# A selective scan inside a four-layer network: outputs kept in the gathered tiles and scattered through four views, gathers moved to the head of each step, last rows written from three tiles

## The chip, the cores and the metric

The kernel runs on one core of a Trainium2 chip. The metric is the device time of one execution in microseconds (us), the median of several runs. The core has five engines that work side by side, each through its own queue in order: PE (TensorE, matmuls), DVE (VectorE), ACT (ScalarE), POOL (GpSimd) and SP (SyncE, which here only issues DMAs). An instruction waits at the head of its queue until the semaphores it needs are up, and everything behind it on that engine waits too.

## The reference, cut to what matters

The input is one image of 1024 channels and 64 x 64 = 4096 pixels. Four residual layers follow, each `x = x + layer(groupnorm(x))`: a mixing layer with a decay along the channels (L0), a 1x1 convolution (L1), a gated state-space layer (L2), another 1x1 convolution (L3). The change lies in L2:

```python
xz = silu(in_proj_w @ x + in_proj_b)            # 3072 channels
x_ssm, res, gate = split(xz, 3)                 # 1024 each
xf = silu(depthwise_conv3(x_ssm))               # along the 4096 pixels
dt, B, C = split(dbc_w @ xf + dbc_b)            # per head: 1, 8 and 8 rows; dt = softplus(dt)
x_h, dt, B, C = gather(..., perm[head])         # pixels in another order, per head
for t in pixels:                                # state h: 512 x 8 per head
    h = exp(dt[t] * A) * h + dt[t] * B[t] * x_h[t]
    y[t] = h @ C[t]
y = gather(y + D * x_h, inverse(perm))          # back to the pixels' order
out = silu(out_proj_w @ (y * silu(gate) + res) + out_proj_b)
```

There are 2 heads of 512 channels and 8 states.

## The kernel before, in words

All 1024 x 1024 products are done by a seven-product scheme on halves of the matrices (`multiply`): per pair of pixel blocks, two groups of seven products, each product two half-products of 8 matmul records. Their operands are the normalized image (`b11`, `b21`, `b22`, from ACT at L943) and differences of it (`t1` to `t4`, made at L797 by DVE or POOL).

**The stage before the scan (WX).** The x_ssm product runs over four pairs of blocks. `conv` (L1054) and `turn` (L1075) follow it: each block is convolved, transposed and written as 512-byte pieces of rows to the DRAM tensor `tok_d` (L1098), one row per pixel and head: 512 channels, then the parts of C and B and dt. `finish(pair)` (L1144) takes the dt, B and C of one pair of blocks from `acc`: softplus of dt, B times dt (L1185), and then, for every lot of four 128-pixel tiles, the split of B and C into a high and a low part (L1198, L1200 on DVE; the second copies L1201, L1202 on POOL) into one tile `row`, which is written to `tok_d` by SP (L1205 to L1210). There is a single `row`, so the next lot's first write (L1191 on DVE) waits until the DMA of the lot before has landed. Between two lots of a pair the generator yields once, that is for one product's time; in the last pair (`finish(NP - 1)`, nine tiles: two lots of four and one of one) there is nothing between.

**The scan.** The 4096 pixels of each head are taken in 74 chunks (`NK`) of 56 pixels, the two heads in one tile of 128 partitions. For each chunk k:
- `gather(k)` (L1289): an indirect DMA from POOL brings 128 rows of `tok_d` into the tile `g` (6 buffers). It is asked for at the end of step k - 5.
- `step_sums`, `turn_rows`, `spread_decay`: `ds` on ACT (L1299), two small products `pr` on PE (L1305, L1306), then `bts`, `E`, `cd` on DVE (L1312 to L1320).
- `cross` (L1327, `pg` on PE), the Exp of `E` on ACT (L1384), `weigh` (L1335, L1337, L1340: the 128 x 128 matrix `G` on DVE).
- `apply(k)`: `py = G' g` on PE (L1344); ACT copies the 8 state rows of each head from `py` into the next chunk's `g` (L1347), and all of `py` into a tile `y` with 2 buffers (L1349). `py` has one PSUM buffer.
- `scatter(k)` (L1353): an indirect DMA from POOL writes `y` to rows of `y_d`. `y_d` is one DRAM tile, and as its rows are chosen at run time each scatter is ordered behind the one before: POOL waits until that one has landed.

Between these the PE is given the half-products of the next product, WR (`res`), by `next_units`: one or two in each turn of the loop `for k in range(-1, NK + 1)` (76 turns). Eight matmul records make a half-product. Its results go through `rg` tiles: ACT copies them out (L1024), DVE adds (L1028), ACT applies silu four at a time (`activate`, L1034) and SP writes them to `res_d`. 14 half-products are given before the first turn of the loop. `sums`, one piece a turn, forms combinations of two weight matrices on POOL (L468 to L488) with loads and stores on SP (L475, L484, L495).

The order on DVE, PE, POOL and ACT is the order of the program text (`manual_schedule`). The pools of the scan stage (`l2r2` with 6 `rg` tiles, `l2g`, `l2b`, `l2h`) lie where the pools of the WX stage (`l2a`, `l2a2`) lay, so their first writers wait for the last users of those.

After the scan, `two_steps` computes gate, out_proj and L3; `load_y` (L1498) reads `y_d`.

Of the kernel before, what the change touches and what calls it, by code (L numbers as in the profile page):

```python
# [36 lines left out]
NK = -(-N // LT)  # L37
HS = HEADS * S
KW, MW = 4 * HS, 66
NF2 = 9 * HS  # L40
CF, BF, DT = 0, KW, 2 * KW
HI, LO = {CF: (0, 2), BF: (0, 1)}, {CF: (1, 3), BF: (2, 3)}
NSPEC = HEADS * S + 1

W1, WX, WR, WG, WO, W3 = range(6)
# [47 lines left out]
def tile_net(ctx: ExitStack, tc: tile.TileContext, x, par_d, cst_d, w_d, w2_d, dbcw_d, out):  # L93
# [17 lines left out]
    s2_d = {m: dram.tile([7, 7, P, 2 * QO], F32, name=f"s2_{m}_d") for m in (WG, WO, W3)}  # L111
    res_d = dram.tile([C, N], F32, name="res_d")
    tok_d = dram.tile([HEADS * N + NSPEC, DH + NF2], F32, name="tok_d")
    y_d = dram.tile([HEADS * N + P * NK, DH], F32, name="y_d")
    perm_d = dram.tile([HEADS * N, 1], I32, name="perm_d")


# [113 lines left out]
    with tc.tile_pool(name="spec", bufs=1) as sp:  # L231
        rows = sp.tile([NSPEC, DH + NF2], F32, name="spec")
        nc.gpsimd.memset(rows, 0.0)
        for at in (BF, CF):
            for j in HI[at]:
# [265 lines left out]


    mean0 = const.tile([P, CT], F32, name="mean0")
    sum0 = const.tile([P, CT, 2 * NPIECE], F32, name="sum0")
    sq0 = const.tile([P, CT, 2 * NPIECE], F32, name="sq0")
    with tc.issue_after(exp_ln.ins), tc.tile_pool(name="l0x", bufs=2) as lx, \
            tc.tile_pool(name="l0x2", bufs=1) as lx2, \
            tc.tile_pool(name="wsum0", bufs=1, side="right") as wsum0, \
# [30 lines left out]
        for t in range(T0):  # L539
            nc.gpsimd.tensor_scalar(dtm[:, t, :], cst[:, CST["row"]], pcol("dtw", t), None, ALU.mult)  # L540
        carry = l0.tile([P, 2, T0], F32, name="carry", bufs=1)
        nc.vector.memset(sum0, 0.0)
        nc.vector.memset(sq0, 0.0)
        nmean0 = l0.tile([P, CT], F32, name="nmean0", bufs=1)
# [494 lines left out]
    with tc.tile_pool(name="l2a", bufs=2) as pa, tc.tile_pool(name="l2a2", bufs=1) as pa2, \  # L1039
# [104 lines left out]
        def finish(pair):  # L1144
            n = 2 * TPB
            yield
            acc = accs[pair].rearrange("p b (h f) -> p b h f", h=HEADS)
            if pair == NP - 1:

                nc.vector.memset(acc[:, n], 0.0)  # L1150
                nc.scalar.activation(end, end, AF.Silu)
                pe = ps_tp("end_pt")
                nc.tensor.transpose(pe[:CT, :P], end, ident)
                et = pa.tile([CT, P], F32, name="end_t", bufs=1)
                nc.scalar.copy(et, pe[:CT, :P])
                for h in range(HEADS):
                    nc.sync.dma_start(tok_d[h * N + N - 1 : h * N + N, :DH].rearrange("a (b c) -> (a b) c", c=P),
                                      et[h * KH : (h + 1) * KH, :])
                pz = ps_tp("end_dbc")
                for o in range(CT):  # L1160
                    nc.tensor.matmul(pz[:1, : HEADS * NF], end[:, o : o + 1], both[:, o, P:], start=(o == 0), stop=(o == CT - 1))
                nc.vector.tensor_tensor(accs[pair][:1, n], pz[:1, : HEADS * NF], dbcb[:1], ALU.add)
                n += 1


            def t(name):
                w = pa.tile([P, 2 * TPB + 1, HEADS], F32, tag=f"sp_{name}", name=f"sp_{name}{pair}", bufs=1)
# [12 lines left out]
            nc.vector.reciprocal(v, u)  # L1180
            nc.vector.tensor_tensor(d, d, v, ALU.mult)
            nc.scalar.activation(u, u, AF.Ln)
            nc.vector.tensor_tensor(u, u, d, ALU.add)
            nc.vector.tensor_tensor(u, u, m, ALU.add)
            nc.vector.tensor_tensor(f[:, :, :, 1 : 1 + S], f[:, :, :, 1 : 1 + S],  # L1185
                                    u.unsqueeze(3).to_broadcast([P, n, HEADS, S]), ALU.mult)
            for b0 in range(0, n, TPB):
                if b0:
                    yield
                q = min(TPB, n - b0)  # L1190
                nc.vector.tensor_copy(row[:, :q, :, DT], u[:, b0 : b0 + q])  # L1191
                for h in range(HEADS):
                    for at, c in ((BF, 1), (CF, 1 + S)):
                        v = f[:, b0 : b0 + q, h, c : c + S]
                        parts = row[:, :q, h, at : at + KW].rearrange(
                            "p b (a c) -> p b a c", c=HS)[:, :, :, h * S : (h + 1) * S]
                        (hi, hi2), (lo, lo2) = ([parts[:, :, j] for j in which[at]] for which in (HI, LO))
                        nc.vector.tensor_scalar(hi.bitcast(I32), v.bitcast(I32), 12, 12, ALU.logical_shift_right,  # L1198
                                                ALU.logical_shift_left)
                        nc.vector.tensor_tensor(lo, v, hi, ALU.subtract)  # L1200
                        nc.gpsimd.tensor_copy(hi2, hi)  # L1201
                        nc.gpsimd.tensor_copy(lo2, lo)  # L1202
                    t0 = pair * 2 * FB + b0 * P - 1
                    if t0 < 0:
                        nc.sync.dma_start(tok_d[h * N : h * N + P - 1, DH:], row[1:, 0, h, :])  # L1205
                        nc.sync.dma_start(tok_rows(t0 + P, q - 1, NF2, DH, h), row[:, 1:q, h, :])
                    elif q < TPB:
                        nc.sync.dma_start(tok_d[h * N + N - 1 : h * N + N, DH:], row[:1, 0, h, :])
                    else:
                        nc.sync.dma_start(tok_rows(t0, q, NF2, DH, h), row[:, :q, h, :])  # L1210

        forget(LATE)
        with tc.manual_schedule(engines={E_.DVE, E_.PE, E_.Pool, E_.Activation}):
# [47 lines left out]
            while ready or due or due2 or due3:  # L1261
                follow()
                next_units(8)
                next_units(8)
                follow_on()
                next_units(8)
                activate(len(silus))
            for _ in finish(NP - 1):
                pass

# [3 lines left out]

    with tc.tile_pool(name="l2r2", bufs=6) as prg, tc.tile_pool(name="l2g", bufs=6) as pgat, tc.tile_pool(name="l2b", bufs=2) as pb, tc.tile_pool(name="l2h", bufs=1) as ph, \
            tc.tile_pool(name="ps2b", bufs=1, space=PSUM) as psb:
        rg_pools[:] = [prg] * 6 + rg_pools * 4
        G2 = [ph.tile([P, P], F32, name=f"G{i}") for i in range(2)]  # L1280
# [60 lines left out]

        def apply(k):
            py = psb.tile([P, FB], F32, tag="y", name=f"py{k}")
            nc.tensor.matmul(py, G2[k % 2], rows.pop(k)[:, :DH], start=True, stop=True)  # L1344
            if k + 1 < NK:
                for h in range(HEADS):
                    nc.scalar.copy(rows[k + 1][h * LC : h * LC + S, :DH], py[h * LC : h * LC + S])  # L1347
            y = pb.tile([P, DH], F32, tag="y", name=f"y{k}")
            nc.scalar.copy(y, py)  # L1349
            return y  # L1350

        def scatter(k, y):
            nc.gpsimd.indirect_dma_start(  # L1353
                out=y_d[:, :], out_offset=bass.IndirectOffsetOnAxis(ap=dst_[:, k : k + 1], axis=0),
                in_=y[:, :], in_offset=None,
            )

        sums = (None for m in (WO, W3) for _ in sum_weights2(m, ph, nc.sync, 64, lag=(1, None)))
# [3 lines left out]

        pgs = {}
        with tc.manual_schedule(engines={E_.DVE, E_.PE, E_.Pool, E_.Activation}):
            while given < first:
                next_units(total)
            for k in range(5):
                gather(k)
            step_sums(0)
            for k in range(-1, NK + 1):  # L1370
                upto = first + (k + 2) * (total - first) // (NK + 2)
                turned = turn_rows(k + 1) if k + 1 < NK else None
                if k > 0:
                    weigh(k - 1, pgs.pop(k - 1))
# [446 lines left out]
```

## Time and profile before

| | |
|---|---|
| median of 3 runs | 2718.75 us (2718.61 to 2720.78) |
| the profiled execution | 2721.77 us, span 2719.4 us |
| PE / DVE / ACT / POOL busy | 95% / 67% / 40% / 45% of the span |
| DMA | 598.22 MB, mean 220 GB/s |
| scan stage, 1142.54 to 1649.50 us | 506.96 us, PE busy 482.92, DVE 365.57, ACT 325.29, POOL 311.88 |
| `g` gathers, `y_d` scatters | 74 each, 964 and 1012 ns on POOL each |

In the group and timeline lines, `out<-in` are the program's names, `x74` a count; the brackets or the last columns hold the idle time of the engine just before and what ended it. An ended wait is named by the instruction or the DMA that came last. A timeline line can hold several instructions, merged. "PEclk" is the share of full clock that PE was granted in a stretch.

### The profile page before, as it was taken

Reading aid. Unit: us, or ns where it says so; the run is one execution under the profiler, and the core shown is the slowest. Engines: PE = TensorE matmul, PEld = TensorE weight load, DVE = VectorE, ACT = ScalarE, POOL = GpSimd, SP = SyncE. Lnnn points to the kernel's source line nnn. Section 1 sums busy time; section 2 is a strip of 40 time slices with the busy share of each in tenths; the row PEclk is TensorE's granted clock in tenths of the full one; section 3 lists DMA queues with packets and bytes.
Section 4 is the critical chain, followed back from the end, with each engine's and each line's share of the span. In section 5 each row is a group of like instructions: output and inputs, shape, how many; then the busy total and the mean of one; then the engine's idle time right before and its main releaser. Section 6 shows DMA issues by size and latency. Waiting matters only on the chain.

```text
span 2719.4 us, 30951 instructions
## 1 busy us (share of the span) xinstructions
PE 2577.5 (95%) x9520; PEld 1715.8 (63%) x9520; DVE 1824.2 (67%) x3870; ACT 1086.4 (40%) x1840; POOL 1223.9 (45%) x1166
## 2 busy tenths in 40 slices
PE   4788999999999999999999999999999999999999
PEld 3664444444555555444444447888888888788887
DVE  6996856655555644377777775577576686877777
ACT  3783110103646554375766554322233133321220
POOL 4154123232122220246585665566575565654544
PEclk9897999999999999999999999999999999999999
DMA  7245467546443363478888994879799898788896
GB/s 287 102 169 201 147 218 262 190 124 230 139 138 103 110 175 111 144 236 262 236 236 236 277 269 152 242 244 305 217 278 292 235 308 238 248 304 292 299 328 215
DMA packets 423577, 598.22 MB, mean 220 GB/s; under 512 B 141909, under 2 KB 211669, under 8 KB 420342
## 3 DMA queue, kind: packets, MB, share of 16 engines
q1 hardware_dynamic: 299062, 368.89, 42.3%
q10 hardware_dynamic: 91456, 136.33, 14.3%
q0 software_dynamic: 32896, 91.04, 12.9%
q8 instruction: 77, 1.26, 0.2%
q14 instruction: 86, 0.70, 0.1%
HBM read 435.63 MB, written 160.51 MB: 219 GB/s over the span
## 4 chain that ended last, share of the span: by engine, by line
PE 48%; DVE 3%; DMA 2%; issue 2%; ACT 2%; POOL 1%; SPq 0%; DVEq 0%; POOLq 0%; ACTq 0%
PE mm L839 8%; PE q_P2P L1695 5%; PE q_P6P L1695 5%; PE q_P5P L1695 5%; PE q_P3P L1695 5%; PE q_P7P L1695 5%; PE q_P1P L1695 5%; PE q_P4P L1695 5%; PE py L1344 2%; DMA y_d<-y,dst 1%; POOL s L468 1%; PE pr L1305 1%; DMA g<-tok_d,src 0%; DVE pg L1337 0%; DVE t L797 0%
## 5 line engine op out<-in xcount | busy, mean ns | idle before, releaser
L839 PE MATMUL mm<-t,w 128*128 128x512 f32 x1536 | 687.4, 598 | 9.3 <-ACT rg L1024 6.2
L839 PE MATMUL mm<-b,w 128*128 128x512 f32 x1152 | 518.7, 602 | 4.0 <-ACT b L943 2.9
L839 PEld LDWEIGHTS mm<-t,w 128*128 128x128 f32 x1536 | 287.4, 191 | 335.2 <-issue 315.6
L839 PEld LDWEIGHTS mm<-b,w 128*128 128x128 f32 x1152 | 218.0, 193 | 254.7 <-issue 243.7
L1664 ACT COPY qQ<-q_P5P 128x512 f32<-128x512 f32 x48 | 28.1, 585 | 294.9 <-PE q_P5P L1695 294.9
L1065 DVE SCALAR_TENSOR_TENSOR cvp<-xs,par,cvp 128x512 f32<-128x512 f32 x128 | 95.3, 754 | 71.7 <-ACT cvp L1062 69.4
L1353 POOL DMA_INDIRECT y_d<-y,dst x74 | 74.9, 1012 | 143.2 <-ACT y L1349 83.5
L468 POOL TENSOR_TENSOR s<-s 128x256 f32<-128x256 f32 (+3 forms) x120 | 130.0, 1090 | 7.9
L1092 POOL TENSOR_TENSOR acc<-l2xt,acc 128x136 f32<-128x136 f32 x56 | 27.2, 486 | 234.6 <-ACT l2xt L1086 233.6
L1116 DVE TENSOR_TENSOR xs<-mm,xs 128x512 f32<-128x512 f32 x64 | 41.9, 685 | 125.0 <-PE mm L839 125.0
L1347 ACT COPY g<-py 8x512 f32<-8x512 f32 x146 | 83.6, 573 | 77.4 <-PE py L1344 69.5
L958 DVE SCALAR_TENSOR_TENSOR image<-mm,par,image 128x512 f32<-128x512 f32 x64 | 47.2, 746 | 95.6 <-PE mm L839 95.6
L1084 PEld LDWEIGHTS l2pt<-both,cv 128*128 128x128 f32 x512 | 77.6, 192 | 34.6 <-issue 24.2
L1335 DVE TENSOR_TENSOR E<-E,pg 128x512 f32<-128x512 f32 x74 | 50.5, 683 | 69.1 <-PE pg L1327 63.5
L797 POOL TENSOR_TENSOR t<-t,b 128x512 f32<-128x512 f32 x40 | 55.6, 1416 | 90.7 <-DVE t L797 90.6
L943 ACT ACTIVATE b<-image,gnl_bias,gnl_r_r 128x512 f32<-128x512 f32 x48 | 36.9, 807 | 143.8 <-PE mm L839 122.4
L1695 PE MATMUL q_P1P<-t_b,wq_P1P 128*128 128x256 f32 x384 | 92.5, 385 | 1.9 <-POOL t_b L1459 1.9
L1463 ACT ACTIVATE qb<-x_x_b,gn_bias,gn_r_r 128x512 f32<-128x512 f32 x64 | 48.8, 807 | 109.2 <-DVE qQ L1625 37.3
L1695 PE MATMUL q_P4P<-t_t,wq_P4P 128*128 128x256 f32 x384 | 90.9, 380 | 1.3 <-DVE qV L1672 1.3
L797 POOL TENSOR_TENSOR t<-b,t 128x512 f32<-128x512 f32 x60 | 76.2, 1294 | 35.4 <-DVE t L797 35.3
L1695 PE MATMUL q_P5P<-t_t,wq_P5P 128*128 128x256 f32 x384 | 90.8, 379 | 0.0
L1695 PE MATMUL q_P6P<-t_t,wq_P6P 128*128 128x256 f32 x384 | 90.7, 379 | 0.0
(418 smaller groups left out, 5972.5 us busy)
## 6 DMA issues: line engine op xcount, KB each, us to landing
w<-s_d SPq DMA_DIRECT2D x96, 512.0 KB
w<-in_w_dram SPq DMA_DIRECT2D x72, 512.0 KB
x_x_b<-x_d ACTq DMA_DIRECT2D x28, 1024.0 KB
image<-x_d SPq DMA_DIRECT2D x12, 2048.0 KB
wq_P6P<-s_d SPq DMA_DIRECT2D x84, 256.0 KB
wq_P7P<-s_d SPq DMA_DIRECT2D x84, 256.0 KB
wq_P5P<-s_d SPq DMA_DIRECT2D x84, 256.0 KB
wq_P3P<-s_d SPq DMA_DIRECT2D x84, 256.0 KB
```

Of the source, the lines that this page charges most:

```text
L468: eng.tensor_tensor(out, a, b, ALU.subtract)
L797: eng.tensor_tensor(B[name][k], B[one][k], B[two][k], ALU.subtract)
L839: nc.tensor.matmul(to[o], w[:, k, o * P : (o + 1) * P], B[name][k], start=(fresh and k == 0), stop=(k == KH - 1), skip_group_check=True)
L958: nc.vector.scalar_tensor_tensor(part, ps, pcol(bias_name, o), part, ALU.add, ALU.add)
L1065: nc.vector.scalar_tensor_tensor(cv, xo[:, at + t : at + t + FB], pcol("dww", 3 * o + t), cv, ALU.mult, ALU.add)
L1084: nc.tensor.matmul(pt[:, q * NV : (q + 1) * NV], cv[:, (q0 + q) * P : (q0 + q + 1) * P], both[:, o, :], start=True, stop=True)
L1335: nc.vector.tensor_tensor(Ef, Ef, pg, ALU.mult)
L1344: nc.tensor.matmul(py, G2[k % 2], rows.pop(k)[:, :DH], start=True, stop=True)
L1347: nc.scalar.copy(rows[k + 1][h * LC : h * LC + S, :DH], py[h * LC : h * LC + S])
L1353: nc.gpsimd.indirect_dma_start(out=y_d[:, :], out_offset=bass.IndirectOffsetOnAxis(ap=dst_[:, k : k + 1], axis=0), in_=y[:, :], in_offset= ...
L1463: nc.scalar.activation(tile_of(j, name)[:, k], held[j, "x", name][:, k], AF.Identity, bias=bias, scale=scale)
L1695: nc.tensor.matmul(ps[:, o, :], w[:, k, o * P : (o + 1) * P], rhs[:, k, :], start=(new and o == 0 and k == 0), stop=(k == 1), skip_group_c ...
```

## The change

1. `y_d` becomes a DRAM tensor outside the pools, and the scatters write in turn through four views of it that the dependency tracker takes as disjoint: a scatter is no longer ordered behind the one before. (Reads of `y_d` still are behind all of them.)
2. `apply` copies `py` into the first 512 columns of the gathered tile `g` of its own chunk, which nothing reads any more; the tile `y` is gone. `g` has 8 buffers for 6. So `gather(k + 5)`, which takes over the tile of chunk k - 3, is behind `scatter(k - 3)`.
3. `gather(k + 5)` stands at the head of turn k, before `turn_rows`, not at the end behind `scatter(k - 1)`; the first five stand before the half-products that are given ahead of the loop (13 for 14), with one `activate(4)` among these.
4. In `finish`, the split of C comes before the softplus, that of B after it; both copies of a part are written by one DVE instruction (its input is broadcast), so the POOL copies are gone. Between two lots of a pair there are two yields for one. In the last pair the lots are 4, 3 and 2 tiles, each in a tile of its own (`row`, and two `spare` tiles in the buffers of `xs`, cleared by POOL), and the writes of head 1 are issued by POOL, those of head 0 by SP.
5. A row of `tok_d` is 642 numbers for 656 (`NF2` 130 for 144); the pools of the scan stage are in another order; `sum0` and `sq0` lie in the first layer's pool.

```diff
-NF2 = 9 * HS
+NF2 = 2 * KW + 2
...
-    y_d = dram.tile([HEADS * N + P * NK, DH], F32, name="y_d")
+    y_d = nc.dram_tensor("y_rows", (HEADS * N + P * NK, DH), F32, kind="Internal").ap()
...
+            lots = [(0, TPB, row), (TPB, TPB, row)]
+            if pair == NP - 1:
+                lots = [(0, TPB, row), (TPB, 3, spare[0]), (TPB + 3, n - TPB - 3, spare[1])]
+
+            def split(b0, q, to, at, c):
+                for h in range(HEADS):
+                    x = f[:, b0 : b0 + q, h, c : c + S].unsqueeze(2).to_broadcast([P, q, 2, S])
+                    parts = to[:, :q, h, at : at + KW].rearrange(
+                        "p b (a c) -> p b a c", c=HS)[:, :, :, h * S : (h + 1) * S]
+                    hi, lo = parts[:, :, HI[at]], parts[:, :, LO[at]]
+                    nc.vector.tensor_scalar(hi.bitcast(I32), x.bitcast(I32), 12, 12, ALU.logical_shift_right,
+                                            ALU.logical_shift_left)
+                    nc.vector.tensor_tensor(lo, x, hi, ALU.subtract)
...
+            for i, lot in enumerate(lots):
+                if i == 0 or lot[2] is not row:
+                    split(*lot, CF, 1 + S)
...
-            for b0 in range(0, n, TPB):
-                if b0:
+            for i, (b0, q, to) in enumerate(lots):
+                if i and to is row:
                     yield
-                q = min(TPB, n - b0)
-                nc.vector.tensor_copy(row[:, :q, :, DT], u[:, b0 : b0 + q])
+                    yield
+                    split(b0, q, to, CF, 1 + S)
+                split(b0, q, to, BF, 1)
+                nc.vector.tensor_copy(to[:, :q, :, DT], u[:, b0 : b0 + q])
...
-                        nc.gpsimd.tensor_copy(hi2, hi)
-                        nc.gpsimd.tensor_copy(lo2, lo)
...
+                    dma = nc.gpsimd if h and pair == NP - 1 else nc.sync
...
-            total, first, given = NP * 2 * NG * 7, 14, 0
+            total, first, given = NP * 2 * NG * 7, 13, 0
...
-    with tc.tile_pool(name="l2r2", bufs=6) as prg, tc.tile_pool(name="l2g", bufs=6) as pgat, tc.tile_pool(name="l2b", bufs=2) as pb, tc.tile_pool(name="l2h", bufs=1) as ph, \
+    with tc.tile_pool(name="l2g", bufs=8) as pgat, tc.tile_pool(name="l2b", bufs=2) as pb, tc.tile_pool(name="l2r2", bufs=6) as prg, tc.tile_pool(name="l2h", bufs=1) as ph, \
...
+        y_views = dram_disjoint_views(y_d[:, :], 4)
...
-            nc.tensor.matmul(py, G2[k % 2], rows.pop(k)[:, :DH], start=True, stop=True)
+            nc.tensor.matmul(py, G2[k % 2], rows[k][:, :DH], start=True, stop=True)
...
-            y = pb.tile([P, DH], F32, tag="y", name=f"y{k}")
+            y = rows.pop(k)[:, :DH]
             nc.scalar.copy(y, py)
...
-                out=y_d[:, :], out_offset=bass.IndirectOffsetOnAxis(ap=dst_[:, k : k + 1], axis=0),
-                in_=y[:, :], in_offset=None,
+                out=y_views[k % len(y_views)][:, :], out_offset=bass.IndirectOffsetOnAxis(ap=dst_[:, k : k + 1], axis=0),
+                in_=y, in_offset=None,
...
+            for k in range(5):
+                gather(k)
             while given < first:
                 next_units(total)
-            for k in range(5):
-                gather(k)
+                if len(silus) > 3:
+                    activate(4)
             step_sums(0)
             for k in range(-1, NK + 1):
                 upto = first + (k + 2) * (total - first) // (NK + 2)
+                if 4 < k + 5 < NK:
+                    gather(k + 5)
...
-                if 4 < k + 5 < NK:
-                    gather(k + 5)
```

More of the change, by code (lines that the diff above doesn't have):

```diff
@@ L7 @@
 from concourse import mybir
+from concourse.ap import dram_disjoint_views
 from concourse._compat import with_exitstack
@@ L39 @@
 KW, MW = 4 * HS, 66
-NF2 = 9 * HS
+NF2 = 2 * KW + 2
 CF, BF, DT = 0, KW, 2 * KW
-HI, LO = {CF: (0, 2), BF: (0, 1)}, {CF: (1, 3), BF: (2, 3)}
+HI = {CF: slice(0, 3, 2), BF: slice(0, 2)}
+LO = {CF: slice(1, 4, 2), BF: slice(2, 4)}
 NSPEC = HEADS * S + 1
@@ L234, in tile_net @@
         for at in (BF, CF):
-            for j in HI[at]:
+            for j in range(KW // HS)[HI[at]]:
                 c = DH + at + j * HS
@@ L503, in tile_net @@
     mean0 = const.tile([P, CT], F32, name="mean0")
-    sum0 = const.tile([P, CT, 2 * NPIECE], F32, name="sum0")
-    sq0 = const.tile([P, CT, 2 * NPIECE], F32, name="sq0")
     with tc.issue_after(exp_ln.ins), tc.tile_pool(name="l0x", bufs=2) as lx, \
@@ L541, in tile_net @@
         carry = l0.tile([P, 2, T0], F32, name="carry", bufs=1)
+        sum0 = l0.tile([P, CT, 2 * NPIECE], F32, name="sum0", bufs=1)
+        sq0 = l0.tile([P, CT, 2 * NPIECE], F32, name="sq0", bufs=1)
         nc.vector.memset(sum0, 0.0)
@@ L1186, in finish @@
                                     u.unsqueeze(3).to_broadcast([P, n, HEADS, S]), ALU.mult)
-            for b0 in range(0, n, TPB):
-                if b0:
+            for i, (b0, q, to) in enumerate(lots):
+                if i and to is row:
                     yield
-                q = min(TPB, n - b0)
-                nc.vector.tensor_copy(row[:, :q, :, DT], u[:, b0 : b0 + q])
-                for h in range(HEADS):
[L1193 to L1200, printed above, removed]
-                        nc.gpsimd.tensor_copy(hi2, hi)
-                        nc.gpsimd.tensor_copy(lo2, lo)
-                    t0 = pair * 2 * FB + b0 * P - 1
@@ L1204, in finish @@
+                    yield
+                    split(b0, q, to, CF, 1 + S)
+                split(b0, q, to, BF, 1)
+                nc.vector.tensor_copy(to[:, :q, :, DT], u[:, b0 : b0 + q])
+                t0 = pair * 2 * FB + b0 * P - 1
+                full = min(q, 2 * TPB - b0)
+                for h in range(HEADS):
+                    dma = nc.gpsimd if h and pair == NP - 1 else nc.sync
                     if t0 < 0:
-                        nc.sync.dma_start(tok_d[h * N : h * N + P - 1, DH:], row[1:, 0, h, :])
@@ L1206, in finish @@
-                        nc.sync.dma_start(tok_rows(t0 + P, q - 1, NF2, DH, h), row[:, 1:q, h, :])
-                    elif q < TPB:
-                        nc.sync.dma_start(tok_d[h * N + N - 1 : h * N + N, DH:], row[:1, 0, h, :])
-                    else:
-                        nc.sync.dma_start(tok_rows(t0, q, NF2, DH, h), row[:, :q, h, :])
+                        dma.dma_start(tok_d[h * N : h * N + P - 1, DH:], to[1:, 0, h, :])
+                        dma.dma_start(tok_rows(t0 + P, q - 1, NF2, DH, h), to[:, 1:q, h, :])
+                    else:
+                        dma.dma_start(tok_rows(t0, full, NF2, DH, h), to[:, :full, h, :])
@@ L1212, in tile_net @@
+                    if full < q:
+                        dma.dma_start(tok_d[h * N + N - 1 : h * N + N, DH:], to[:1, full, h, :])
         forget(LATE)
@@ L1267, in tile_net @@
                 activate(len(silus))
+            spare = []
+            for i in range(2):
+                w = pa.tile([P, 2 + 2 * FB], F32, tag="xs", name=f"row{i}", bufs=4)[:, : 3 * HEADS * NF2]
+                nc.gpsimd.memset(w, 0.0)
+                spare.append(w.rearrange("p (b h c) -> p b h c", b=3, h=HEADS))
             for _ in finish(NP - 1):
```

## The prediction, made before the changed kernel ran

> **What bounds the kernel now.** I read the page's slices first: PE is busy 95% of the span, in tenths 9 in nearly every slice, so time can only come from stretches in which PE stands or is clocked down. Then I took the stretches in one table (bounds, length, busy time and count of PE, PEld, DVE, ACT and POOL, granted clock, DMA share, GB/s): the scan, its start, and one late stretch.
>
> ```profile
> 1142.54:1649.50 506.96, 482.92 (x1318) 237.03 (x1318) 365.57 (x811) 325.29 (x564) 311.88 (x319) 0.98 0.82 245
> 1136.30:1142.60 6.30, 0.11 (x2) 0.06 (x1) 2.51 (x15) 0.70 (x2) 2.24 (x13) 0.72 0.55 177
> 1545.30:1552.12 6.82, 6.67 (x12) 3.11 (x11) 4.34 (x10) 2.66 (x7) 4.17 (x4) 0.50 1.05 361
> ```
>
> In the scan PE lacks only 24.0 of 507 us. The second row is the start: PE does almost nothing for 6.3 us. The third shows a second loss, hidden in busy time: at clock 0.50 for 6.82 us PE does half the work, 3.41 us lost. In undisturbed turns of the timeline a half-product (8 records) takes 3.49 us and the scan's own products (two `py` 0.86, `pg` 0.24, `pr` 0.50) 1.60. So a turn with one half-product is 5.08 us, 54 of 76 turns are such, and 74 x 1.60 + some 100 x 3.49 = 467 us is a floor; the stage is 40 above it, 24 as idle and 16 in stretches of half clock and slower neighbours. Then PE's waits from 1090 us:
>
> ```profile
> PE pr L1306 <- ACT ds L1299: 9.5, 7, 2.9
> PE mm L839 <- ACT rg L1024: 6.2, 1, 6.2
> PE py L1344 <- DVE G L1340: 4.0, 5, 2.0
> PE py L1344 <- ACT y L1349: 3.1, 4, 2.1
> PE mm L839 <- POOL t L797: 2.9, 2, 1.9
> ```
>
> ACT stands ahead of most of it. So ACT's waits in 1142 to 1650 us, and POOL's:
>
> ```profile
> ACT g L1347 <- PE py L1344: 69.5, 41, 6.0
> ACT y L1349 <- DMA y_d<-y,dst: 48.2, 21, 6.4
> ACT ds L1299 <- DMA g<-tok_d,src: 23.9, 16, 5.8
> ```
>
> ```profile
> POOL y_d L1353 <- ACT y L1349: 83.5, 24, 14.0
> POOL y_d L1353 <- DMA y_d<-y,dst: 18.9, 7, 3.5
> ```
>
> The copy into `y` waits 48.2 us, in 21 of 74 steps, for the scatter that frees its buffer. POOL's long wait for ACT is the other side of it. One case, on ACT:
>
> ```profile
> 1575.39 0.58 ACT L1349 COPY y<-py 128x512 f32<-128x512 f32 x1 [5.38 <-DMA y_d<-y,dst]
> ```
>
> Last, DVE: the writer of `row` in the first pair of WX, and in the last pair.
>
> ```profile
> 805.81 0.17 DVE L1191 COPY row<-sp_u 128x8 f32<-128x8 f32 x1 [5.17 <-DMA tok_d<-row]
> ...
> 1140.05 0.17 DVE L1191 COPY row<-sp_u 128x2 f32<-128x2 f32 x1 [2.39 <-DMA tok_d<-row]
> ```
>
> **Part by part.** The sum is made against the profiled execution, 2721.77 us (span 2719.4), which is 3.0 above the median.
>
> *Scatters unordered, no tile `y` (1, 2).* A scatter lands 2.7 to 7.2 us after its issue, median 4.7. Ordered, one follows another by landing plus some 0.6 us, so about 5.3, above the 5.08 of a turn: in a run of single turns scatters fall behind until ACT stops. I walked PE's gaps in the scan and added the half clock behind each (a stretch is 3.41 us long, so 1.71 lost):
> - 1457.44: `ds` 2.86 late, behind a `y` copy that waited 2.02 and a lot of silus. 2.02 + 1.71 = 3.73. (The other 0.84 is the silus' and stays.)
> - 1542.89: `py` 2.07 late behind a `y` copy that waited 4.45, then the 6.82 us above: 2.07 + 3.41 = 5.48.
> - 1571 to 1579: four gaps, 1.92 + 0.46 + 0.50 + 2.22 = 5.10 (two of them behind waits of 5.4 us).
> - 1314 and 1315: `g` 0.73, `ds` 1.39 and half clock 1.71 = 3.83: a gather that was asked for late, behind a waiting scatter.
> - Two small ones, 0.36 + 0.30 = 0.66.
>
> That is 18.8. At 1346 and 1366 (0.38 + 2.02 + 1.71 = 4.11) the chain runs through a gather and through loads of `w` behind `s_d`, which stay: half, 2.05. Together 20.9. What is late next? DVE has 385 us of work over 76 turns, 5.07 a turn against PE's 5.08, and the gaps before `G` (4.0 us in the waits) are its own. ACT's lots of silus with a table load (3.84 us in one piece) stay too. With stalls gone they have less room, so I let a third come back: **-13.9**. Bounds: 0, if all of it returns, and -20.9.
>
> Here the Trainium skill speaks against the size. "TensorE: Matmul & The Clock Gate", section "HAM oscillation — how this bites in real kernels", puts the loss of clock at PE-idle gaps above about 3.4 us. No gap inside the scan is so long (at most 2.86). By the rule the clock losses are not the gaps' doing and stay: then 2.02 + 2.07 + 5.10 + 2.12 + 0.66 + 1.20 = 13.2, two thirds of it 8.8, and the sum below is -15.5 with 2703. By the rows a 2.07 us gap that ended at 1544.96 was followed from 1545.30 by clock 0.50, and gaps of 2.86, 2.02 and 1.39 by 3.41 us each, within 0.7 to 1.5 us. I take the rows.
>
> The ACT copy itself costs the same 0.585 us. POOL's issue stays 1.01 a scatter.
>
> *Gather at the head of the turn (3), a new wait.* `gather(k+5)` now waits for `scatter(k-3)`, and behind it on POOL stand the turn's `t`, `sums` and `scatter(k-1)`. Two scatters were issued since, so at 5.08 a turn it has more than 7.6 us (two turns less some 2.5 us of POOL's issues) to land; the longest took 7.2. I put this at nothing. If cover is gone it is the rival "slower". The gather is asked for earlier by the scatter's wait and still five turns ahead of its use, against a landing of 3.5 to 8.3 us: nothing is late for that. POOL has 312 busy of 507 us.
>
> *Last pair of WX and the start (3, 4).* Before: 6.19 us idle to 1142.54, then half clock until 1145.94: in all 6.19 + 1.65 = 7.84. The first `rg` copy had waited 13.1 us for the row DMAs and the last row instructions, and these twice for `row` (1.61 and 2.39). After: C's split (12 instructions, some 2.0 us) lies beside ACT's softplus and table loads, which end near 1127.7, so DVE is done with all three lots near 1131.8 (0.8 a lot from 1129.5, plus what lies between). SP and POOL issue until about 1133.8; row DMAs landed in 2.4 to 4.4 us, so `rg`'s memory is free near 1137.3 (1136 to 1138.5). PE ends its half-product near 1136.35: a gap of about 0.9. Then 13 half-products leave only one before the first `pr`. POOL's memsets (1.74) stand before the first gather, and from that gather's issue to `ds` before took 3.7 us, so `ds` is ready some 5.5 us after the free memory, 2.0 beyond the one half-product. With half of a half-clock stretch (0.85): 0.9 + 2.0 + 0.85 = 3.75, net **-4.1**. Bounds: -1.5 (rows land at 1138.5 and a whole stretch of half clock) and -6.
>
> "DMA: Bandwidth & Descriptors", section "Issuing engines are not separate DMA queues", says that spreading DMAs over engines saves only issue time; its latency table puts a first byte from POOL's path near 1 us, from SP's near 0.6. By the rule, head 1 by POOL would save SP's issues (0.36 to 0.66 each by the trace, three of them) and lose some 0.4 at the end: -3.7. By the trace no plain row DMA from POOL is to be seen near here; POOL took 0.54 to 0.59 for a direct issue elsewhere, so I keep -4.1.
>
> *Two yields (4).* In pair 0 the wait of 5.17 above holds back the next block's convolution; PE stands 3.00 us at 808.76, with half clock behind it (1.71): 4.7. A second yield is one more product, some 7 us, more than the 5.17. **-4.0**; bounds 0 (the wait moves to a later block) and -4.7. Later pairs show no PE gap there: nothing.
>
> *Nothing.* Broadcast splits have 64 numbers for 32 (0.19 us becomes perhaps 0.22; 24 such in a pair, 0.7, under PE's products; if not, +0.7 once). POOL's copies gone: POOL has room. Rows of 2568 B for 2624 are 2% fewer bytes. `sum0`, `sq0`: no time.
>
> Sum: -13.9 - 4.1 - 4.0 = -22.0; 2721.8 - 22.0 = 2699.8, less 3.0: **2697 us**.
>
> **Rivals.**
> - *The stalls are handed on* to DVE, to ACT's lots or to `s_d` (20%). For it: DVE's 5.07 a turn and 8.8 us of such gaps now. Against: DVE is busy 366 of 507 us. Half the sum: 2708.
> - *All of it goes* (20%), `G`'s chain and the clock too: -20.9 - 2 - 6 - 4.7 = -33.6: 2685.
> - *Slower* (4%): POOL, held at the head of turn k by `scatter(k-3)`. The loop is landing plus 2.5 us in two turns; it decides from a sustained landing of 7.6 us, which more scatters in flight at once could give. At 9.5 a turn is 6.0, +0.92 x 53 = +49 less the 8 of WX: 2760; a third of the turns so: about 2727. For it: DMA share .82, 1.05 in the third stretch. Against: median 4.7.
> - *It doesn't do what it says* (3%): scatters still ordered by one queue, `row` not the limit: 2715 to 2719.
>
> **Chances.** Main case 53%, own range 2691 to 2703. About 0.2% (5.4 us) is what a measurement of this kernel can tell from no change. Handed on wholly gives "same"; slower comes from the POOL loop alone with a little for the unknown: faster 0.92, same 0.04, slower 0.04. The range 2685 to 2709 takes in the bounds of the first two rivals.
>
> **What would show it.** Right: no wait of the ACT copy for `y_d`, and none of POOL's scatter for the scatter before; no PE gap at 808 and at most 3 us near 1137; fewer stretches of clock 0.50 in the scan. Gaps before `G` that grow past 4.0 us speak for the first rival. A wait of the gather for `y_d` of more than a few us in sum speaks for the slower one. Wrong would be the step "a third comes back" if the gaps behind `y` go and the stage is still within 5 us of 507.

## The result, and the profile after

The changed kernel takes 2711.66 us (median of 22 runs, 2704.11 to 2715.32), the kernel before 2716.38 in the same set: ratio 0.9984, 95% interval 0.9976 to 0.9992. That is 0.16% faster, between 4 and 5 us. The forecast was 2697, range 2685 to 2709.

The profiled execution took 2715.32 us, span 2713.4. It is the slowest of the 22, 3.7 us above their median, and that of the kernel before lies 5.4 above its own, so the stages below are good to a few us only. Stage by stage against before: the last half-product ahead of the scan ends 3.2 us earlier (1133.19 for 1136.35), the scan's first one begins 5.6 earlier (1136.92 for 1142.54), and the scan then takes 504.3 for 507.0. So of the 13.9 us expected in the scan 2.6 are there. What follows the scan takes 1072.2 for 1069.9, with 3.4 us more at half clock.

In the changed kernel the lines of the scan are L841 (`mm`), L1310 (gather), L1318 (`ds`), L1324 and L1325 (`pr`), L1363 (`py`), L1366 and L1368 (ACT's copies), L1372 (scatter), and L470, L479, L490 for the sums on POOL. The stretches, with the same columns as before: the scan, the gap at its start, and a late stretch.

```profile
1136.92:1641.24 504.32, 480.57 (x1318) 238.50 (x1318) 364.08 (x811) 326.36 (x564) 311.22 (x316) 0.98 0.80 246
1133.10:1136.95 3.85, 0.12 (x2) 0.04 (x1) 0.74 (x2) 0.67 (x2) 0.60 (x4) 1.00 0.10 20
1611.40:1618.23 6.83, 6.10 (x10) 3.25 (x11) 2.16 (x6) 3.70 (x8) 0.96 (x1) 0.50 0.89 353
```

PE stands still for 23.7 us in the scan where it stood for 24.0, and the stretches at clock 0.50 are there again: 23.9 us of the scan for 20.5. What PE waited for from 1080 us:

```profile
PE pr L1324 <- DMA g<-tok_d,src: 9.2, 2, 5.1
PE py L1363 <- DVE G L1359: 6.7, 4, 2.8
PE mm L841 <- POOL t L799: 4.1, 2, 3.2
PE mm L841 <- ACT rg L1026: 3.7, 1, 3.7
PE pr L1325 <- ACT ds L1318: 2.6, 3, 0.9
```

The wait behind the `y` copy has gone, and that behind `ds` is 2.6 us for 9.5. In their place PE waits for gathered rows, 9.2 us in two waits (1.5 before), for `G` 6.7 us (4.0 before) and for `t` from POOL 4.1 us (2.9 before). ACT (first fence) and POOL (second) in the scan:

```profile
ACT g L1366 <- PE py L1363: 92.6, 52, 6.0
ACT ds L1318 <- DMA g<-tok_d,src: 45.9, 18, 8.0
...
ACT g L1366 <- DMA y_rows<-g,dst: 1.5, 2, 1.2
```

```profile
POOL s L490 <- DMA s_d<-s: 48.4, 15, 6.5
POOL y_rows L1372 <- ACT g L1368: 34.1, 14, 7.5
POOL s L479 <- DMA s<-in_w_dram: 18.0, 5, 4.1
POOL g L1310 <- PE pr L1325: 18.0, 9, 4.2
POOL g L1310 <- issue: 14.3, 20, 5.3
POOL y_rows L1372 <- ACT E L1407: 13.1, 5, 11.9
```

ACT waits for a scatter 1.5 us in all, where it waited 48.2: the change does what it says. But ACT's wait for gathers has doubled (45.9 for 23.9), and POOL is now held by two things that held it little before: the sums wait 48.4 us for their own stores (17.7 before), and the gather waits. The names beside the gather's waits (PE `pr`, "issue") are engines that had long been done. Set beside the landings in the trace, the 14 gathers that waited longest, 39.6 us together, all began 0.73 to 0.77 us after the scatter of chunk k - 3 had landed. POOL around the longest of these waits, and PE's wait next to it:

```profile
1313.48 1.13 POOL L490 TENSOR_TENSOR s<-s 128x448 f32<-128x448 f32 x1 [3.20 <-DMA s_d<-s]
1314.69 3.57 POOL L470 TENSOR_TENSOR s<-s 128x448 f32<-128x448 f32 x3
1318.40 0.98 POOL L1310 DMA_INDIRECT g<-tok_d,src  x1
1319.69 0.99 POOL L1372 DMA_INDIRECT y_rows<-g,dst  x1 [0.30 <-issue]
1320.98 0.97 POOL L1310 DMA_INDIRECT g<-tok_d,src  x1 [0.30 <-PE mm L841]
1322.26 0.99 POOL L1372 DMA_INDIRECT y_rows<-g,dst  x1 [0.30 <-issue]
1328.52 0.97 POOL L1310 DMA_INDIRECT g<-tok_d,src  x1 [5.27 <-issue]
```

```profile
1326.00 0.98 PE L1324 MATMUL pr<-cst,g 128*128 128x192 f32 x2 [4.02 <-DMA g<-tok_d,src]
```

The scatter issued at 1319.69 is that of chunk 23; it landed at 1327.79, and the gather of chunk 31 (1328.52) could not go before. By the order of the program text one scatter and one gather lie between `scatter(k - 3)` and `gather(k + 5)`, and in the trace it is so in all 64 cases from chunk 10 on. POOL was late and did these two back to back, so it came to the gather 3.6 us after the scatter's issue.

PE's wait at 1326.00 is not for this gather but for that of chunk 29, issued at 1318.40. That one did not wait for a scatter: it stood behind a piece of the sums, whose two halves had waited 4.08 us for a load and 3.20 us for a store. The same chain (3.95 and 3.03 us) stands ahead of PE's other long wait, 5.14 us to 1612.13. PE's next in length, 3.19 us for `t` to 1539.61, does have a gather's wait ahead of it: POOL was at work without a stop from this gather to that `t`.

```profile
1531.82 0.97 POOL L1310 DMA_INDIRECT g<-tok_d,src  x1 [1.44 <-issue]
```

So POOL is late by two kinds of waits, for scatters and in the sums, and the trace alone does not say which of them matters.

A measure for this is the lag, from the end of ACT's copy of an output to the issue of its scatter: before 6.3 us on average over chunks 10 to 67, after 9.3, nearly two turns. It tells how late POOL is, not what that costs: the runs below do not stand in the order of their lags.

### The profile page after: what moved, and what is told of

The parts are those of the page before. It is cut to its first block, busy times and chain, and to the rows that moved or that the text cites. A ratio compares the mean times of both kernels' runs of the same rounds, so it can differ in the third digit from the quotient of the medians.

```text
span 2713.4 us, 30641 instructions
## 1 busy us (share of the span) xinstructions
PE 2578.7 (95%) x9520; PEld 1718.4 (63%) x9520; DVE 1817.8 (67%) x3870; ACT 1086.8 (40%) x1839; POOL 1218.4 (45%) x1100
## 3 DMA queue, kind: packets, MB, share of 16 engines
q0 software_dynamic: 33104, 91.04, 13.1%
## 4 chain that ended last, share of the span: by engine, by line
PE 45%; DMA 6%; DVE 2%; ACT 2%; POOL 1%; SPq 1%; issue 1%; ACTq 0%; POOLq 0%; DVEq 0%
PE mm L841 7%; PE q_P6P L1716 5%; PE q_P5P L1716 5%; PE q_P7P L1716 5%; PE q_P4P L1716 5%; PE q_P2P L1716 5%; PE q_P3P L1716 5%; PE q_P1P L1716 4%; PE py L1363 1%; DMA s_d<-s 1%; DMA x_x_b<-x_d 1%; POOL s L470 1%; DMA s<-in_w_dram 1%; DMA g<-tok_d,src 1%; DMA x_x_Z<-x_d 1%
## 5 line engine op out<-in xcount | busy, mean ns | idle before, releaser
L841 PE MATMUL mm<-t,w 128*128 128x512 f32 x1536 | 694.4, 603 | 7.9 <-POOL t L799 4.1
L841 PE MATMUL mm<-b,w 128*128 128x512 f32 x1152 | 515.1, 598 | 4.0 <-ACT b L945 2.9
L841 PEld LDWEIGHTS mm<-t,w 128*128 128x128 f32 x1536 | 289.7, 193 | 337.0 <-issue 318.4
L841 PEld LDWEIGHTS mm<-b,w 128*128 128x128 f32 x1152 | 216.4, 192 | 253.0 <-issue 240.7
L470 POOL TENSOR_TENSOR s<-s 128x256 f32<-128x256 f32 (+3 forms) x120 | 130.1, 1091 | 7.9
L1366 ACT COPY g<-py 8x512 f32<-8x512 f32 x146 | 83.9, 574 | 95.0 <-PE py L1363 92.6
L1372 POOL DMA_INDIRECT y_rows<-g,dst x74 | 73.5, 993 | 66.5 <-ACT g L1368 34.1
L1086 PEld LDWEIGHTS l2pt<-both,cv 128*128 128x128 f32 x512 | 76.5, 190 | 32.6 <-issue 23.9
L1310 POOL DMA_INDIRECT g<-tok_d,src x74 | 72.1, 974 | 52.9 <-PE pr L1325 18.0
L1480 POOL TENSOR_TENSOR t_t<-qt 128x512 f32<-128x512 f32 x23 | 29.6, 1289 | 137.6 <-DVE qt L1480 77.8
```

The costliest lines, as they stand in the source:

```text
L470: eng.tensor_tensor(out, a, b, ALU.subtract)
L841: nc.tensor.matmul(to[o], w[:, k, o * P : (o + 1) * P], B[name][k], start=(fresh and k == 0), stop=(k == KH - 1), skip_group_check=True)
L1086: nc.tensor.matmul(pt[:, q * NV : (q + 1) * NV], cv[:, (q0 + q) * P : (q0 + q + 1) * P], both[:, o, :], start=True, stop=True)
L1310: nc.gpsimd.indirect_dma_start(out=g[:, :], out_offset=None, in_=tok_d[:, :], in_offset=bass.IndirectOffsetOnAxis(ap=src[:, k : k + 1], ax ...
L1372: nc.gpsimd.indirect_dma_start(out=y_views[k % len(y_views)][:, :], out_offset=bass.IndirectOffsetOnAxis(ap=dst_[:, k : k + 1], axis=0), i ...
```

## The experiments

**First theory: the scan's gain went into POOL's queue.** Rivals: WX and the start had not gained what the trace shows; unordered scatters land later and POOL's own work is the bound; the sums alone hold POOL. Four runs.

*oldscan*: 13 half-products ahead; tile `y`, 6 buffers of `g` and one view again, gather at the end of the loop's body (its two lines at the head taken out).

```diff
-        y_views = dram_disjoint_views(y_d[:, :], 4)
+        y_views = [y_d[:, :]]
...
-            y = rows.pop(k)[:, :DH]
+            rows.pop(k)
+            y = pb.tile([P, DH], F32, tag="y", name=f"y{k}")
...
                 if len(silus) > 3:
                     activate(4)
+                if 4 < k + 5 < NK:
+                    gather(k + 5)
```

> The changed kernel with the scan's data path as before: tile y with 2 buffers, 6 buffers of g, gather at the end of the turn, scatters ordered. What is left of the change is WX, the last pair and the start. Theory 1 (the scan part gained nothing because POOL now falls behind: its gather waits for scatter(k-3), and late gathers stop PE in place of late copies): WX and start stand alone with about -7 us, so 2709 to 2710 and a ratio near 0.9974; the scan again near 507 us with waits of the ACT copy for y_d above 40 us. Theory 2 (WX and start gain little, the scan some): 2712 to 2716.

*ytile_gend*: the same with the four views kept.

> As the run above, but scatters through four views: so before's layout with unordered scatters. Theory 1: gathers no longer stand behind scatters, copies into y wait less; gather waits for y rows gone, scan 495 to 501 us, 2700 to 2706. Theory 3 (unordered scatters land later and POOL's own work with the sums is the bound, wherever the gather stands): scan 503 to 507, 2708 to 2712.

*gend*: the changed kernel, only the gather moved to the end of the loop's body.

> The changed kernel with the gather back at the end of the turn, so behind a scatter that is a turn older, and asked for a turn later. Theory 1: POOL's waits of the gather for scatters fall from some 45 us to under 15 and its lag with them; 2704 to 2709. If only the time of asking counts (the lead of the gather), it is slower than the change: 2714 to 2720.

*latesums*: the changed kernel without `next(sums, None)` in the loop, so that all pieces come after the scan.

> The changed kernel with all pieces of sums after the scan (the total gets longer, by waits for the weights; only the scan stage is to be read). Theory 1: POOL still waits for scatter(k-3), its lag behind the ACT copy stays at 5 us or more, the scan stays at 500 us or more. Theory 4 (it is the waits of the sums for their own loads and stores, 66 us, that hold POOL back): the lag falls under 3 us, ds waits for g under 15 us, the scan is at most 494 us.

Measured: oldscan 2755.61 us (ratio 1.0150, 1.0134 to 1.0166), ytile_gend 2718.30 (1.0013, 1.0004 to 1.0022), gend 2715.61 (1.0005, 0.9996 to 1.0014). All three missed what the first theory expected (gend came where its rival, the time of asking, had put it), and the reason is partly mine: I had taken "the end of the turn", as the text ahead of the prediction also calls it, for the gather's old place. In the kernel before it in fact stands directly behind the scatter, ahead of the turn's second half-product with its `t` and ahead of the sums; in these three runs it stood behind both. So they say something else: behind `t` and the sums a gather is asked for too late. ACT's `ds` waits 77.9 us for gathers in gend and 102.0 in oldscan.

latesums was clear. Its total, 2971.16, is longer since the weights come late, and is not to be read; its scan is:

```profile
1136.00:1619.08 483.08, 472.03 (x1318) 234.83 (x1318) 362.45 (x811) 324.82 (x564) 192.27 (x188) 0.99 0.59 197
```

483.1 us for 504.3, without one stretch of half clock after its start, and `ds` waits 4.1 us for gathers. The theory that the sums hold POOL back took this one. It can't tell their waits from their 119 us of work on POOL and their transfers.

**Second theory: it is when the sums are done.** The number of half-products given ahead of the loop (13 for 14) had entered my sum only as cover for the start. But the turns in which a piece of the sums is skipped are chosen by `given // 2 % 14 != 12`. With 13, turn 6 is no longer skipped, the pieces come a turn earlier, and the second half of a piece (4.7 us, which waits for the store of the first) falls into a turn with four `t` (5.0 us). Four runs:

```diff
before13 (the kernel before)
-            total, first, given = NP * 2 * NG * 7, 14, 0
+            total, first, given = NP * 2 * NG * 7, 13, 0
first14 (the changed kernel), oldscan14 (oldscan)
-            total, first, given = NP * 2 * NG * 7, 13, 0
+            total, first, given = NP * 2 * NG * 7, 14, 0
phase (the changed kernel)
-                if given // 2 % 14 != 12:
+                if (given + 1) // 2 % 14 != 12:
```

> The kernel before with 13 half-products ahead of the loop for 14, nothing else. That number also sets, through the skipped turns, in which turns POOL does the pieces of sums: a turn earlier, so that a second half of a piece (4.7 us, and a wait for its own store) falls into a turn with four t (5.0 us). Theory 5 (this phase is what holds POOL back and cost the oldscan run its 39 us): 2740 to 2760. Theory 4 without the phase (sums hold POOL wherever they stand) or any other cause in oldscan: 2714 to 2722.

> The oldscan kernel with 14 half-products ahead of the loop. Theory 5: back to WX and start alone, 2706 to 2712. If the 39 us come from the order of pools, the first gathers or the DRAM tensor: 2745 to 2756.

> The changed kernel with 14 half-products ahead of the loop, nothing else. Theory 5: the scan gains what was predicted for it, stage about 490 to 497 us, 2696 to 2704. Otherwise 2709 to 2714.

> The changed kernel with 13 half-products, but the skipped turns counted as if there were 14, so that the pieces of sums stand a turn later. Theory 5: as with 14, 2696 to 2706; if the number of half-products itself counts (PE and the first gathers), 2709 to 2714.

| | us | ratio to before, 95% |
|---|---|---|
| before13 | 2730.00 | 1.0049 (1.0036 to 1.0063) |
| oldscan14 | 2744.54 | 1.0110 (1.0095 to 1.0124) |
| first14 | 2698.17 | 0.9926 (0.9914 to 0.9939) |
| phase | 2699.09 | 0.9935 (0.9922 to 0.9948) |

One number costs the kernel before 13.7 us, less than the theory's 24 to 44, and gives the changed kernel back 13 us; phase, with 13 kept ahead and only the sums moved, does the same, so in the changed kernel it is their turns and not the number (in the kernel before the two were not parted). In oldscan14 28 us stay: they belong to the late gather (wxonly14 below differs from it by the gather's place alone and takes 34 us less).

**What each part of the change is worth**, now with 14 ahead and the gather's true old place:

```diff
                     scatter(k - 1, y)
+                if 4 < k + 5 < NK:
+                    gather(k + 5)
                 next_units(upto)
```

*wxonly14* has tile `y`, 6 buffers of `g`, one view and this place; *views14* the same with four views; *gather14* is the changed kernel with this place; *oneview14* the changed kernel with one view and the gather at the head.

> With 14 half-products ahead; the scan's data path and its order as in the kernel before (tile y, 6 buffers of g, ordered scatters, gather directly behind the scatter, ahead of the sums; the earlier oldscan runs had put it behind the sums). WX, last pair and start alone. If these stand alone with the 7 us that the trace shows up to the scan: 2707 to 2711. If most of the 18 us of the 14-ahead version comes from them: 2698 to 2703.

> As the run above with the four views: unordered scatters out of tile y. If it is the order among the scatters that cost time before: 2699 to 2704, waits of the ACT copy for y rows under 15 us. If the tile y with its 2 buffers stays a limit: 2705 to 2711.

> The changed kernel with 14 ahead and the gather directly behind the scatter, so behind POOL's wait for the ACT copy. If the head of the turn is worth something (ds waits less for g): 2700 to 2706. If not: 2696 to 2700.

> The changed kernel with 14 ahead and one view: scatters in order, outputs kept in g with 8 buffers, gather at the head. ACT no longer waits for a scatter, but POOL does. If freeing ACT from the scatter is what counts: 2697 to 2702. If the order among scatters is (POOL late, gathers late): 2706 to 2715.

| | us | ratio to before, 95% |
|---|---|---|
| wxonly14 | 2710.48 | 0.9980 (0.9971 to 0.9988) |
| views14 | 2694.61 | 0.9922 (0.9905 to 0.9940) |
| gather14 | 2693.38 | 0.9917 (0.9900 to 0.9933) |
| oneview14 | 2740.71 | 1.0093 (1.0077 to 1.0110) |

The last three came outside both of their expected ranges. WX, last pair and start give 6 us (with the narrower rows and the order of the pools, which wxonly14 also has). The views give 16 more, with tile `y` still there. Keeping the outputs in `g` adds nothing that these runs can tell (gather14 against views14), and neither does the head of the turn (first14 against gather14). With outputs in `g`, ordered scatters and the gather at the head it is 24 us slower than before. POOL in that run:

```profile
POOL y_rows L1372 <- DMA y_rows<-g,dst: 53.8, 18, 6.1
```

Freed of the two buffers of `y`, ACT runs ahead and POOL falls 13.1 us behind on average, 25 at worst: that the tile `y`, which stops ACT after two outputs, had also kept POOL from falling further behind is argued from this, not tried apart.

**What was still open: is the head of the turn part of the cost, and where is it lost?** Three runs on the changed kernel with 13 ahead. *phaseA* and *phaseB* move the sums in one stretch of the scan each, *gather13* puts the gather behind the scatter.

```diff
-                if given // 2 % 14 != 12:
+                if k not in (6, 7, 28, 50, 71, 72):
...
+                if k not in (7, 28, 29, 49, 50, 71):
```

(The first added line, in place of the removed one, is phaseA's, the second phaseB's; the skipped turns of the changed kernel are 7, 28, 29, 50, 71 and 72.)

> The changed kernel, 13 ahead; only the pieces of sums in turns 7 to 28 stand a turn later, so that the first half of a piece and not the second shares turn 12 with four t. If the loss is made there (POOL 14 us late at chunk 11, stops of PE near 1322 us): two thirds or more of the 13 us come back, 2698 to 2703. If it is made in the later stretch: 2709 to 2712.

> As above, but only the pieces in turns 49 to 71 stand a turn later (POOL 17 us late at chunk 54, stops of PE near 1537 and 1607 us). If the loss is made there: 2698 to 2703; if each stretch has its share: 2704 to 2707 here and in the run above; if the first has it: 2709 to 2712.

> The changed kernel, 13 ahead, with the gather directly behind the scatter as in the kernel before. If the gather at the head, waiting for scatter(k-3) ahead of t and scatter(k-1), is part of the loss: 2698 to 2705. If the phase alone makes it, wherever the gather stands: 2708 to 2713.

Measured: phaseA 2708.06 (0.9970, 0.9958 to 0.9981), phaseB 2701.30 (0.9943, 0.9927 to 0.9959), gather13 2696.99 (0.9923, 0.9906 to 0.9939). The later stretch makes most of the loss, about 10 us; the 4 us of the first are hardly clear of the noise (its interval overlaps that of the change, 0.9976 to 0.9992). The two moves together are *phase*, 2699.09. Their lags do not follow the times: 6.5 us in phaseA, 8.4 in phaseB, the faster one. And gather13 gets all of it back with the sums in their bad turns. Its scan, and then POOL's waits in it:

```profile
1139.27:1625.95 486.68, 474.08 (x1318) 235.56 (x1318) 362.68 (x811) 325.53 (x564) 311.95 (x316) 0.99 0.82 255
```

```profile
POOL y_rows L1372 <- ACT g L1368: 74.8, 26, 13.3
POOL s L490 <- DMA s_d<-s: 28.2, 12, 5.2
POOL s L479 <- DMA s<-in_w_dram: 26.2, 5, 7.7
POOL g L1310 <- issue: 15.4, 51, 0.3
...
POOL g L1310 <- PE py L1363: 2.7, 3, 2.1
```

Only one gather still waited for its scatter, 0.8 us, where they had waited 39.6: behind the scatter two scatters and two gathers lie between `scatter(k - 3)` and `gather(k + 5)`, and POOL came to the gather at least 6.1 us after that scatter's issue (3.5 in the change). POOL waits 74.8 us for ACT's copies, where it waited 34.1: it is on time more often. The lag is 4.0 us for 9.3. The sums wait less for their own stores too (28.2 for 48.4) in the very same turns, while their waits for loads grew (26.2 for 18.0); that a POOL which is not catching up leaves more time between a piece's halves is my reading, not shown. And the gathers, although they stand later in the text, go out earlier before their use: 9.1 us from the end of the issue to `ds` on average, 8.5 in the changed kernel.

Last, two runs: *head4* asks for `gather(k + 4)` at the head for `gather(k + 5)`; *gphase* is gather13 with the line of phase.

> The changed kernel, 13 ahead, gather(k+4) at the head of turn k for gather(k+5): the same place, but it waits for scatter(k-4), a turn older, and is asked for a turn later. If the wait for scatter(k-3) is what holds POOL: gather waits for scatters well under half of the 45 us, 2695 to 2702. If the place itself costs, or the shorter lead stops PE: 2708 to 2716.

> The changed kernel, 13 ahead, gather directly behind the scatter, and the pieces of sums a turn later. If the phase only costs where POOL is held at the head: 2694 to 2698, as gather13. If both add up: 2686 to 2691.

head4 took 2717.22 (1.0006, 0.9995 to 1.0016), gphase 2695.80 (0.9927, 0.9912 to 0.9942). head4 can't answer its question: the head of the next turn is the end of this one on POOL, so its order is that of gend again, behind `t` and the sums, and it repeats that result (`ds` waits 78.2 us for gathers, the gather for scatters hardly at all). gphase answers: with the gather behind the scatter and unordered scatters the sums' turns make no difference.

So the two edits cost nothing that these runs can tell one at a time, and 18 us together:

| ratio to before | sums as with 14 ahead | sums as with 13 ahead |
|---|---|---|
| gather behind the scatter | gather14 0.9917 | gather13 0.9923 |
| gather at the head | first14 0.9926 | the change 0.9984 |

In first14 the gathers wait just as long for scatters (43.3 us) as in the change, and still it is 13 us faster; POOL's lag is 6.5 us there. It seems to have room for one of the two losses, which fits these four runs but is argued from them. Whether it is the wait at the head or the mere exchange of gather and scatter in POOL's queue was not parted: a ninth buffer of `g`, which would take away the wait alone, was not run.

## Why the prediction missed, step by step

**WX, last pair and start (-8.1): right in kind, some 2 us too much.** By the medians of wxonly14 and before it is 6.6. The wait of 5.17 us on `row` and the gap at 808 are gone: from a gap near 642 us that both traces have, PE gains 4.3 up to its last half-product (4.0 expected). The start gave less. Its gap is 3.73 us where about 0.9 was reckoned, since the rows took 5.0 to 6.1 us to land, not 2.4 to 4.4; 0.57 at the first `pr` follows, and PE works 3.4 us at half clock after the gap, as before. That is 1.9 us of the 4.1.

**Scatters unordered (-13.9): right, in mechanism and size, where nothing else holds POOL.** views14 against wxonly14 is 15.9 us, and the scan of views14 takes 486.3 us for 502.4. ACT's copies waited 17.7 us for scatters there (43.4 in wxonly14), and not at all in gather14, with outputs in `g`. In the change itself all but 2.6 us of the forecast gain is missing by the traces; 504.3 us is within the 5 us of 507 that the prediction named as the sign against "a third comes back". That gather13 takes 2697.0 us, just the forecast, is in part luck: it is 19.2 us below before in its set, not 22, and the parts were off to both sides.

**"I put this at nothing", the gather's new wait: wrong, and this is the step that failed.** The sum was 7.6 us of cover against a landing of at most 7.2. Both sides were off. "Two scatters were issued since" is not so: by the program text it is one, and the two turns less POOL's issues fit the gather behind the scatter, as in gather13. For a POOL on time the cover at the head is one turn and one issue with its gap, 5.1 and 1.3, some 6.4 us (an estimate from the trace's turns and issues); for a POOL that catches up, with scatters 2.6 us apart, it was as little as 3.5, and under 7.6 in 21 of 64 gathers. Landings were longer as well: 8.7 us at most, median 5.9. So 14 gathers waited 39.6 us. With the sums in the turns of 14 this does no harm (first14); with those of 13 it belongs to the 18 us.

**The half-products ahead (13 for 14): a term that the sum did not have.** I used it for the start and did not ask what else reads that counter. It moves the sums by a turn. It and the gather at the head make the loss together, neither of them alone.

**The rivals.** The mechanism of the one called slower, POOL held at the head by `scatter(k-3)`, was the one that came, at 4%. Its point of decision was wrong: no sustained landing of 7.6 us was needed, only a POOL that was late for another reason. Its sign, a wait of the gather for `y_d` above a few us, is there with 39.6, but does not decide: it is there with 43.3 in first14, which is not slow. The rival that the stalls are handed on named 2708 and was nearest in time, but to DVE, ACT's lots or `s_d`. They went to POOL's gathers, and in part to `s_d`: the sums' waits for their stores there went from 17.7 to 48.4 us and stand in the chains of PE's two longest waits in the scan. Its sign came too, gaps before `G` of 6.7 us for 4.0. DVE's 5.07 us a turn, its ground, counts overlapping instructions twice; the busy time in the first row of the prediction, 365.57 us, is 4.81 a turn.

**The clock.** I had weighed the rows against the rule of the Trainium skill ("TensorE: Matmul & The Clock Gate", "HAM oscillation — how this bites in real kernels") of gaps above 3.4 us. The rows hold: in the changed kernel the gap of 5.14 us to 1612.13 reaches into the third stretch shown above, as the rule would have it, but gaps of 2.80 (to 1487.63) and 3.19 (to 1539.61) were each followed within 1 us by 3.41 us at clock 0.50 too, and in first14 one of 1.79, 1.3 us later. The scan of views14, whose longest gap is 2.01, has none after its start. In the kernel before, the stretches at the gaps of 2.86 and 1.39 us began 0.35 and 0.11 us before the gap ended and that at 2.02 us 0.12 us after it, not the 0.7 to 1.5 us that I read; the point against the rule stands. So neither 3.4 us nor another length parts the gaps that cost clock from those that don't in these traces.

## What to carry to other kernels

An engine that issues DMAs has a budget like any other: add up what it does and everything it waits for in a turn, and reckon every cover for the case that it is late and catching up, when turns follow each other at the pace of its issues. Count in the program text what stands between a wait and the thing it waits for. Two losses that are each harmless can together use up the same slack. When a change touches a counter, look for everything that is scheduled by it.

## What the runs showed of the hardware

With the sums out of the scan (latesums, DMA share 0.59) a scatter landed in 2.75 us (median) and a gather in 4.14; in the changed kernel (0.80) it was 5.9 and 6.1. The share is not all of it: with 0.83 in gather14 scatters landed in 4.5 us and gathers in 6.1, with 0.80 and ordered scatters in wxonly14 in 4.4 and 5.6. How much comes from the traffic and how much from scatters issued close together was not parted. In the changed kernel the 14 indirect DMAs that waited longest for another one started 0.73 to 0.77 us after that had landed.
